# The bias of 128 exponentials on ScalarE: a constant in the instruction instead of a one-column tile

## The chip, the cores and the metric

The kernel runs on one core of a Trainium2 chip. A core has five engines that run side by side and meet only through semaphores: TensorE (matrix products, PE in the profile; its weight loads are PEld), VectorE (DVE), ScalarE (ACT), GpSimd (POOL) and SyncE (SP), which here only issues transfers. Data lie in SBUF (128 partitions) and in PSUM, the banks that TensorE writes. The metric is the device time of one execution in microseconds, as the median of several runs; the profile is of one execution, and its span is a little shorter than the timed run.

## The reference

`x` is 4096 x 64, `adj` is 4096 x 4096 with zeros and ones, and there are a 64 x 64 weight and a bias.

```python
h = jnp.maximum(_layernorm(x, axis=-1), 0.0)
support = h @ weight
mask = (adj != 0).astype(support.dtype)
rank = jnp.cumsum(mask, axis=1)
deg = rank[:, -1:]
k = jnp.minimum(deg, 100.0)
pos = rank - (deg - k)
w = mask * jnp.where(pos > 0, 0.5 ** (k - pos), 0.0)
return x + w @ support + bias
```

So every row of `adj` weights its neighbours by powers of one half. The last neighbours of a row count most when it has over 100 of them, and the exponent of a neighbour is the number of neighbours that follow it in its row (less an excess over 100). The matrix, 64 MB, has to be read once.

## The kernel before

The columns of `adj` are handled in two halves, right one first, since the exponents are counts from the right. The 4096 rows are 32 row tiles of 128; four row tiles make a group (8 groups), and a group with one half of the columns is a *unit* (16 units, 0 to 15). A unit is loaded as four transfers of 1 MB (128 rows x 2048 columns), 64 in all, numbered 0 to 63, all issued from one queue (L120) into a ring of eight buffers.

What becomes of a tile and of a unit, with the names of the functions and the lines that the profile shows:

- *convert* (L341 on VectorE; for tiles 1, 7 and 15 L339 on ScalarE): the ones and zeros become bytes, four matrix columns to a 32-bit word.
- *transpose* (L352, TensorE) turns the words, *settle* (L363, VectorE; L361 for the three tiles above) copies them from PSUM to the tile `mt`.
- *totals* (L369, TensorE) counts neighbours in each run of columns. *split* (L379, ScalarE) and *divide* (L382, VectorE) take two bytes of the counts into one tile `sums`; divide waits for split. *carry* (L388, GpSimd) adds what the right half counted.
- *suffix* (L396, TensorE) sums the counts from the right, and *clamp* (L400, VectorE) limits them.
- *place* (u, a) (L407 and L412, TensorE) makes the exponents of four blocks k of unit u: four products of L407, then sixteen of L412 that finish the four PSUM tiles `v` together. `v` is a ring of five buffers, so the fourth tile of a place can only be begun when the third tile of the place before has been read.
- *weigh* (u, k) (L420, ScalarE) reads two bytes of each word of `v` and writes 2 to the power of minus (byte + 38), 128 x 1024 numbers, to `wk`. This is the exponential. In the last unit, blocks 5, 6 and 7 are weighed in two halves of 128 x 512 each. There are 122 full and 6 half exponentials.
- For three blocks near the end, (14, 4), (15, 0) and (15, 4), VectorE builds the powers instead: *encode* (L426) and *take* (L431); *lower* (L439, GpSimd) prepares the other factor, and their aggregate is called *gather*.
- *aggregate* (L453, TensorE) multiplies `wk` with the rows of `support` in two parts (`hr`) and adds to `acc`, one PSUM tile per group.
- *drain* (L469, ScalarE; L467 on VectorE for the last quarter), *turn_back* (L476, TensorE) and *finish* (L483 and L484, VectorE) bring the sums into rows and add `x`. Two large stores and two small ones write the result (L491, L486).

Ahead of this stands a set-up with the normalisation of `x`, the product with the weight and the small constants. One of them is the tile `floor`, 128 x 1, filled once by GpSimd with -38 ln 2 (L192 and L193).

The order of the work on each engine is written out ahead: a planner at the end of the kernel holds for every task a rank, an estimated duration and its needs, and sorts all tasks into one list. Each engine runs its part of the list in that order and waits by semaphores where an input is not there yet. The estimates (1000 ns for a full exponential, 570 for a half) are not changed by the edit, so the order isn't either.

The line in question is the last one of weigh:

Of the kernel before, what the change touches and what calls it, by code (L numbers as in the profile page):

```python
# [15 lines left out]
U8 = mybir.dt.uint8  # L16
AF = mybir.ActivationFunctionType
# [10 lines left out]
LN2 = 0.6931471805599453  # L28
# [3 lines left out]
def kernel(  # L32
# [34 lines left out]
    nc = tc.nc  # L67
# [124 lines left out]
    floor = const.tile([P, 1], F32, name="floor")  # L192
# [135 lines left out]
    low, codes, masks, words, wts, accs, tots, pts, sums8, behind, vs, signed = {}, {}, {}, {}, {}, {}, {}, {}, {}, {}, {}, (1, 7, 15)  # L328
# [86 lines left out]
    def weigh(u, k, part=None):  # L415
        r = slice(0, W) if part is None else slice(part * W // 2, (part + 1) * W // 2)
        if not part:
            wts[u, k] = wpool.tile([P, 2, W], F32R, name="wk")
        v = vs[u, k] if part == 0 else vs.pop((u, k))
        nc.scalar.activation(wts[u, k][:, :, r], v.bitcast(U8).rearrange("p (i f) -> p f i", f=4)[:, :2, r], AF.Exp, scale=-LN2, bias=floor)  # L420

    def encode(u, k):

# [150 lines left out]
    for u, (g, c0, cb) in enumerate(UNITS):  # L574
# [9 lines left out]
        for k in range(2 * cb):  # L584
            due = at + k
            if k % 4 == 0:
                task(place, (u, k // 4), PE, due, 800, 920, [("clamp", u), ("constants", 1)], ("v", *(("encode" if (u, k + j) in QUICK else "weigh", u, k + j, *((1,) if u == U - 1 and k + j in PARTED else ())) for j in range(4))))
            if u == U - 1 and k in PARTED:
                continue
            weighs = "weigh"  # L590
            piece_of = block(u, k) // (HB // 2)
            if (u, k) in QUICK:
                weighs = "take"
                task(encode, (u, k), DVE, due - 8, 1160, 1300, [("place", u, k // 4), ("convert", NT - 2)])
                task(take, (u, k), DVE, due - 8, 690, 820, [("encode", u, k)], ("w", ("gather", u, k)))
                task(lower, (u, k), POOL, due - 8, 1200, 1300, [("second", piece_of // 2, piece_of % 2), ("convert", NT - 3)])
            else:
                task(weigh, (u, k), ACT, due + 2.5, 1000, 1130, [("place", u, k // 4)], ("w", ("aggregate", u, k)))
            task(gather if (u, k) in QUICK else aggregate, (u, k), PE, due + 14, 480, 720, [(weighs, u, k), ("lower", u, k) if (u, k) in QUICK else None, ("second", piece_of // 2, piece_of % 2)] +
                 ([("drain", g - 1)] if g and head and k == 0 else []))  # L600
        for part in range(2 if u == U - 1 else 0):
            for k in PARTED:
                due = at + k + part
                task(weigh, (u, k, part), ACT, due + 2.5, 570, 700, [("place", u, k // 4)], None if part else ("w", ("aggregate", u, k, 1)))
                task(aggregate, (u, k, part), PE, due + 14, 260, 500, [("weigh", u, k, part)])
# [20 lines left out]
    while kinds:  # L626
        heads = []
        for kind, keys in kinds.items():
            f, args, engine, rank, hold, lag, needs, pool = tasks[keys[0]]
# [10 lines left out]
        f, args, _, _, hold, lag, _, pool = tasks[key]  # L640
# [54 lines left out]
```

## Time and profile before

| | before |
|---|---|
| time, median of 3 runs | 192.47 us (192.40 to 192.48) |
| span of the profiled execution | 190.5 us |
| TensorE busy | 170.0 us (89%) |
| VectorE busy | 161.6 us (85%) |
| ScalarE busy | 160.0 us (84%) |
| exponentials, L420 | 128, 130.5 us busy, 1106 ns mean |
| read from memory | 68.2 MB, 363 GB/s over the span |

Busy time on an engine is the sum of its reported durations; neighbours overlap a little on ScalarE and VectorE, so that a reported duration is longer than the time for which an instruction keeps the engine from the next one. Two instructions back to back tell the latter by the distance of their starts. Where lines of a timeline are shown, the columns are the start in us from the beginning of the span, the length in us of the (merged) piece, engine, line, operation, output and input, shapes and number of instructions; in square brackets stands the idle time just ahead and what ended it. In tables of stretches the columns are: the stretch in us, its length, the busy time of PE, PEld, DVE, ACT and POOL with their numbers of instructions, the granted TensorE clock, the busy share of the 16 DMA engines, and GB/s.

### The profile page before, as it was taken

The page shows a single profiled execution, that of the slowest core. Times are in us where ns is not written, and L with a number is a line of the kernel's source. Part 1 is how long each engine was busy: PE and PEld are TensorE (multiplying, and loading weights), DVE is VectorE, ACT ScalarE, POOL GpSimd, SP SyncE. Part 2 cuts the span into 40 slices and gives each one's busy share as a digit, 9 for nine tenths or more (in the row PEclk, how much of TensorE's full clock was granted, in tenths as well). Part 3 has the DMA queues.
Part 4 walks back from the last instruction along what each step waited for, and adds up shares of the span by engine and source line. Part 5 has one row for each costly group of instructions (what it writes and reads, how often), then busy time and mean ns, then how long its engine had stood idle before and what let it go on. Part 6 is the DMA issues. An engine that isn't in the chain of part 4 may idle for free.

```text
span 190.5 us, 3798 instructions
## 1 busy us (share of the span) xinstructions
PE 170.0 (89%) x1499; PEld 105.3 (55%) x1499; DVE 161.6 (85%) x221; ACT 160.0 (84%) x176; POOL 20.0 (10%) x60
## 2 busy tenths in 40 slices
PE   7779878899979999999899989998898989999980
PEld 5657646465636564556466545563554455655460
DVE  4834886999999999999998999989879879996633
ACT  2298248699999997999998989798977998999980
POOL 7000062300001000100100010000100029001000
PEclk9999999999999999999999999999999999999996
DMA  6999999999999999999999999999999999912000
GB/s 201 420 427 420 415 423 421 418 413 427 420 413 425 420 415 425 420 416 425 420 413 427 420 415 427 418 416 425 418 411 428 418 415 425 381 40 83 0 3 28
DMA packets 10338, 69.49 MB, mean 365 GB/s; under 512 B 1360, under 2 KB 1616, under 8 KB 2128
## 3 DMA queue, kind: packets, MB, share of 16 engines
q1 hardware_dynamic: 10016, 69.15, 87.9%
q8 instruction: 12, 0.20, 0.4%
q10 hardware_dynamic: 304, 0.10, 0.2%
q14 instruction: 6, 0.05, 0.1%
HBM read 68.19 MB, written 1.05 MB: 363 GB/s over the span
## 4 chain that ended last, share of the span: by engine, by line
PE 33%; DVE 33%; DMA 20%; ACT 6%; POOL 3%; issue 2%; POOLq 0%; ACTq 0%; DVEq 0%
DMA a_sb<-in_adj_dram 20%; DVE m L341 16%; PE acc L453 11%; PE pt L352 6%; DVE mt L363 6%; ACT wk L420 4%; PE v L407 3%; PE v L412 3%; PE tot L369 2%; DVE behind L400 2%; DVE sums L382 2%; PE pc L265 1%; PE ps L396 1%; ACT mt L260 1%; DVE xs L307 1%
## 5 line engine op out<-in xcount | busy, mean ns | idle before, releaser
L420 ACT ACTIVATE wk<-v,floor 128x1024 fp32r<-128x1024 uint8 (+1 forms) x128 | 130.5, 1106 | 8.6 <-PE v L412 8.6
L341 DVE TENSOR_SCALAR m<-a_sb 128x2048 uint8<-128x2048 f32 x61 | 84.6, 1391 | 7.1 <-DMA a_sb<-in_adj_dram 7.1
L453 PE MATMUL acc<-wk,hr 128*128 128x512 f32 (+1 forms) x256 | 79.1, 424 | 1.7 <-ACT wk L420 1.1
L453 PEld LDWEIGHTS acc<-wk,hr 128*128 128x128 f32 x256 | 43.1, 188 | 21.0 <-ACT wk L420 6.7
L352 PE MATMUL pt<-ident,m 128*128 128x128 f32 x256 | 39.8, 279 | 7.6 <-DVE m L341 6.3
L363 DVE COPY mt<-pt 128x512 uint32<-128x512 uint32 x61 | 41.3, 680 | 3.8 <-PE pt L352 3.7
L352 PEld LDWEIGHTS pt<-ident,m 128*128 128x128 f32 x256 | 28.9, 141 | 21.8 <-PE acc L453 4.7
L388 POOL COPY sums<-behind 1x512 f16<-1x512 f16 x8 | 6.4, 798 | 132.8 <-ACT sums L379 132.8
L407 PE MATMUL v<-behind,where 32*128 32x512 f16 x128 | 14.8, 383 | 1.8 <-ACT wk L420 0.9
L412 PE MATMUL v<-mt,tri 32*32 32x512 f16 x512 | 14.3, 395 | 0.0
L379 ACT ACTIVATE sums<-tot 128x512 f16<-128x512 uint8 x16 | 9.6, 602 | 2.9 <-PE tot L369 2.8
L382 DVE CAST sums<-tot 128x512 f16<-128x512 uint8 x16 | 10.9, 680 | 1.3 <-ACT sums L379 1.3
L400 DVE TENSOR_SCALAR behind<-ps,excess 128x512 f16<-128x512 f32 x16 | 11.8, 738 | 0.1
L369 PE MATMUL tot<-mt,band 128*32 128x512 f16 x128 | 10.2, 393 | 0.3 <-DVE mt L363 0.3
L412 PEld LDWEIGHTS <-tri 32*32 32x32 f16 x512 | 4.4, 88 | 10.4 <-issue 10.4
L396 PE MATMUL ps<-sums,later 128*128 128x512 f16 x32 | 9.6, 381 | 0.5 <-DVE sums L382 0.5
L407 PEld LDWEIGHTS <-where 32*128 32x128 f16 x128 | 3.7, 91 | 10.0 <-issue 9.3
L339 ACT ACTIVATE m<-a_sb 128x2048 int8<-128x2048 f32 x3 | 7.7, 2560 | 1.2 <-DMA a_sb<-in_adj_dram 1.1
L248 PE MATMUL none<-junk 128*128 128x256 bf16 x44 | 7.6, 351 | 1.1 <-DVE junk L133 1.1
L260 ACT ACTIVATE mt<-px 64x512 f32<-64x512 f32 x8 | 4.2, 586 | 4.8 <-PE px L256 4.8
L248 PEld LDWEIGHTS <-junk 128*128 128x128 bf16 x44 | 5.5, 126 | 3.3 <-DVE junk L133 1.1
L469 ACT ACTIVATE acc_sb<-acc,bias_sb 128x512 f32<-128x512 f32 (+1 forms) x8 | 5.3, 665 | 0.8 <-PE acc L453 0.8
(87 smaller groups left out, 94.1 us busy)
## 6 DMA issues: line engine op xcount, KB each, us to landing
a_sb<-in_adj_dram SPq DMA_DIRECT2D x64, 1024.0 KB, 17.6
xr<-in_x_dram SPq DMA_DIRECT2D x2, 512.0 KB, 6.4
out_dram<-xr SPq DMA_DIRECT2D x1, 512.0 KB, 17.8
out_dram<-xr SPq DMA_DIRECT2D x1, 384.0 KB, 2.3
out_dram<-xr ACTq DMA_DIRECT2D x1, 64.0 KB, 1.6
out_dram<-xr SPq DMA_DIRECT2D x1, 64.0 KB, 1.6
w<-in_L_gnn_weight_dram ACTq DMA_DIRECT2D x2, 16.0 KB, 6.1
bias_sb<-in_L_gnn_bias_dram SPq DMA_DIRECT2D x1, 0.2 KB, 15.9
```

The costliest lines, as they stand in the source:

```text
L248: nc.tensor.matmul(none[:, :2 * P], junk[:, :P], junk, start=True, stop=True)
L341: nc.vector.tensor_scalar(m_v, a_v, 0.0, 64.0, op0=ALU.not_equal, op1=ALU.add)
L352: nc.tensor.transpose(pts[n][:, c, :], m32[:, c * P:(c + 1) * P], ident)
L363: nc.vector.tensor_copy(mw, pt)
L369: nc.tensor.matmul(tot[SUB * c:SUB * (c + 1), :], band[:, SUB - 12 - 4 * a:2 * SUB - 12 - 4 * a], masks[u][:, c, :, a], start=(a == 0), st ...
L382: nc.vector.tensor_copy(*bytes_of(u, 1))
L396: nc.tensor.matmul(px, later[cb][:r, f, :], sums[:r, f, :], start=(f == 0), stop=(f == 1))
L400: nc.vector.tensor_scalar(behind[u], pts.pop((u, "s")), excess[UNITS[u][2]], float(MAX_NEIGH), op0=ALU.subtract, op1=ALU.min)
L407: nc.tensor.matmul(v, where[q, a, :], behind[u][q, :], start=True, stop=False, skip_group_check=True)
L412: nc.tensor.matmul(vs[u, 4 * a + j][SUB * c:SUB * (c + 1), :], tri[q, q], m, start=False, stop=True, skip_group_check=True)
L420: nc.scalar.activation(wts[u, k][:, :, r], v.bitcast(U8).rearrange("p (i f) -> p f i", f=4)[:, :2, r], AF.Exp, scale=-LN2, bias=floor)
L453: nc.tensor.matmul(accs[g][:, r], parts.rearrange("p s d -> p (s d)"), wk[:, s, r], start=(k == s == 0 and c0 + cb * E * P == N), stop=(c0 ...
```

## The change

The activation instruction computes func(scale x input + bias). Its bias can be a column of SBUF with one number for each partition, or a number in the instruction itself. Before, the exponential had the tile `floor`, whose 128 numbers are all -38 ln 2. After, the same number is written into the instruction. The purpose is that ScalarE has one operand less to fetch in each of 128 instructions.

```diff
-        nc.scalar.activation(wts[u, k][:, :, r], v.bitcast(U8).rearrange("p (i f) -> p f i", f=4)[:, :2, r], AF.Exp, scale=-LN2, bias=floor)
+        nc.scalar.activation(wts[u, k][:, :, r], v.bitcast(U8).rearrange("p (i f) -> p f i", f=4)[:, :2, r], AF.Exp, scale=-LN2, bias=-38.0 * LN2)
```

The tile `floor` and its filling stay in the program, unread. Nothing else is edited.

## The prediction

> **What bounds the kernel now.** I read the page's first two parts, then busy time by stretches around the end of the loads, then ScalarE's groups, then the timelines of VectorE and ScalarE from 144 us on, and last the chain of waits in the same stretch.
>
> ```profile
> PE 170.0 (89%) x1499; PEld 105.3 (55%) x1499; DVE 161.6 (85%) x221; ACT 160.0 (84%) x176; POOL 20.0 (10%) x60
> ...
> DMA  6999999999999999999999999999999999912000
> ...
> 160.00:165.00 5.00, 4.78 (x57) 2.85 (x56) 5.00 (x6) 4.37 (x5) 1.85 (x2) 1.00 1.02 424
> 165.00:167.00 2.00, 2.00 (x29) 1.21 (x26) 2.00 (x4) 1.80 (x3) 0.00 (x0) 1.00 0.74 303
> 167.00:168.00 1.00, 1.00 (x5) 0.64 (x4) 1.00 (x2) 1.00 (x2) 0.00 (x0) 1.00 0.19 78
> ```
>
> The first line tempts: ScalarE is 84% busy and the change makes most of its instructions shorter. The second decides: the 16 DMA engines are full from the first slices to about 165 us (share 1.02 at 424 GB/s just before). 64 loads of 1 MB arrive, one each 2.48 us by the landing events of the trace, the last at 167.96 us. No faster engine moves that. So the kernel is a load stream of 168 us and a tail of 22.5 us; only what shortens the tail counts. Three engines are nearly full beside the stream, so one must also ask which of them is late when it ends.
>
> ```profile
> 155.91 0.69 DVE L382 CAST sums<-tot 128x512 f16<-128x512 uint8 x1 [0.86 <-ACT sums L379]
> ...
> 163.87 1.39 DVE L341 TENSOR_SCALAR m<-a_sb 128x2048 uint8<-128x2048 f32 x1
> ...
> 166.34 1.38 DVE L341 TENSOR_SCALAR m<-a_sb 128x2048 uint8<-128x2048 f32 x1
> ...
> 168.87 1.39 DVE L341 TENSOR_SCALAR m<-a_sb 128x2048 uint8<-128x2048 f32 x1
> ```
>
> This is VectorE's timeline. L341 converts a landed tile. The last three convert at 163.87, 166.34 and 168.87 us what landed at 163.00, 165.48 and 167.96: VectorE is 0.9 us behind the stream, and after 155.91 it has no idle time until the last conversion. That idle time of 0.86 us at 155.91 is a wait for ScalarE: divide (L382) may not start before split (L379) of the same unit has ended.
>
> ```profile
> 146.61 6.19 ACT L420 ACTIVATE wk<-v,floor 128x1024 fp32r<-128x1024 uint8 x6 [1.26 <-PE v L412]
> 152.69 0.69 ACT L469 ACTIVATE acc_sb<-acc,bias_sb 128x512 f32<-128x512 f32 x1
> 153.26 2.13 ACT L420 ACTIVATE wk<-v,floor 128x1024 fp32r<-128x1024 uint8 x2
> 155.25 0.62 ACT L379 ACTIVATE sums<-tot 128x512 f16<-128x512 uint8 x1
> ...
> 165.56 6.19 ACT L420 ACTIVATE wk<-v,floor 128x1024 fp32r<-128x1024 uint8 x6 [0.20 <-PE v L412]
> 171.64 0.69 ACT L469 ACTIVATE acc_sb<-acc,bias_sb 128x512 f32<-128x512 f32 x1
> 172.21 1.12 ACT L420 ACTIVATE wk<-v,floor 128x1024 fp32r<-128x1024 uint8 x1
> 173.21 0.61 ACT L379 ACTIVATE sums<-tot 128x512 f16<-128x512 uint8 x1
> 173.68 10.80 ACT L420 ACTIVATE wk<-v,floor 128x1024 fp32r<-128x1024 uint8 x13
> 184.50 0.47 ACT L469 ACTIVATE acc_sb<-acc,bias_sb 128x256 f32<-128x256 f32 x1
> ```
>
> ScalarE's timeline: eight exponentials (L420) in the queue ahead of that late split, and from 165.56 us to the drain (L469) at 184.50 us no idle time at all: 20 exponentials, two other instructions. So ScalarE bounds at two places that count: ahead of 155.25, and in the tail. The chain of waits puts 33% on TensorE, 33% on VectorE and 20% on the loads, and only 6% on ScalarE, since it names whoever came last at each step; near the end it has these lines, with the last five half exponentials on the path:
>
> ```profile
> 181.04 0.46 issue
> 181.49 2.99 ACT wk L420 x5
> 184.48 0.02 issue
> 184.50 0.48 ACT acc_sb L469
> ```
>
> **What the Trainium skill says.** "ScalarE: Activation LUTs", section "What ACT_TABLE_LOAD costs": an activation with constant scale and bias takes 186 ns + 0.833 ns per element, each one-column operand adds about 93 ns, and neighbours overlap by about 93 ns. The trace agrees with the form: 128x1024 with the tile has a median of 1118 ns (280 + 853 = 1133 by the page). "ScalarE activation tables: per-element evaluation and per-set limits", section "What a function is on this engine", says that with the same operands an instruction costs the same whatever the function. The trace agrees: half exponentials and drains, both 512 wide with a bias tile, start 570 and 569 ns ahead of their successor. No page says whether the 93 ns are seen by the next instruction or vanish in the overlap. "Perfetto Trace Analysis", section "Per-instruction lifecycle", says that the reported window runs from the start in the ALUs to the acknowledged write, so the distance of starts is the better measure of what an instruction occupies. I use that.
>
> **The change part by part.** *The operand.* Distances from one start to the next, back to back, in the trace before: exponential of 1024 with the tile 998 ns (median of 90); of 512 with the tile 570; drain of 512 with a bias tile 569; split of 512 (Copy, no tile) 475; turned and relu of 512 (no tile) 477. So at equal width the tile occupies 94 ns, as the page's 93. I take 94 ns: a full exponential goes from 998 to 904 ns, a half from 570 to 476, and the mean reported time of the 128 from 1106 to about 1012 ns. Over 128 that is 12.0 us of ScalarE. Most of it lies beside the full load stream and turns into waits of L420 for L412.
>
> *The tile itself.* The memset of floor stays and is unread (109 ns on GpSimd at 5 us, far ahead of use). The first exponential loses its wait on GpSimd, met 25 us earlier. The order on each engine is otherwise the same; a wait of TensorE on ScalarE stands one instruction group earlier in the set-up (L304 instead of the next L407), on work long done. All of it: 0.
>
> *Ahead of the tail.* Split at 155.25 has eight exponentials before it since ScalarE last waited: 8 x 0.094 = 0.75 us, and 0.07 us more of a small wait on v inside the six: 0.8 us earlier. Its counts (L369) have their last start at 153.21, so they don't hold it. Divide's wait of 0.86 us shrinks by as much, and everything on VectorE after it moves 0.8 us earlier, as does TensorE, whose L407 at 154.44 waits for the exponential of 153.26. The limit is the stream: conversions can move up 0.87 us before they meet their landing. So 0.8 us fits, just.
>
> *In the tail, all 0.8 us earlier to begin with:* exponentials of unit 13 from 164.77. Four at 0.904 end their turn at 168.39; the next needs v of place (14,0), at 169.64 - 0.8 = 168.83. One more to 169.74, one to 170.64: drain. 0.57 later exp (14,2) at 171.21; split of unit 15 at 172.11 (was 173.21; its counts are there at 171.65). Exp (14,3) at 172.59, then three more until 176.2. TensorE: turn_back needs totals and drain: 171.57, then an aggregate; L407 of place (14,1) at 172.5 (was 173.44, -0.94). The order on TensorE (L412, two aggregates, suffix) carries -0.94 to suffix, clamp and place (15,0): L407 at 175.72, v ready at 176.73. Exp (15,1) thus starts at 176.75 instead of 177.81 (-1.06), after half a microsecond of a new wait. The fourth L407 of place (15,1) waits for the end of exp (15,2), the v ring having five buffers: -1.06 - 0.09 - 0.09, so -1.25 at 178.73; v follows 0.93 later, and the half exponentials begin at 179.66 instead of 180.91. Six at 0.476 need 2.86 us where they took 3.59. But VectorE's encode and take of block (15,4) start at the same v and need 2.02 us, to 181.59; gather and two pairs of half aggregates follow on TensorE (1.35 us before, 0.1 of it a wait for ScalarE). Drain at 181.59 + 1.25 + 0.03 = 182.87 instead of 184.50: -1.63. From drain to the end (5.97 us) nothing changes.
>
> Sum: 0.8 (VectorE's late start made good) + 0.8 (tail). 192.47 - 1.6 = 190.9 us.
>
> **The rivals.** (a) *VectorE's lead is lost again.* Another wait between 145 and 160 us, for instance VectorE on transposes (0.57 us at 148.99), takes the place of the one for split. Then the tail starts where it did: place (15,0) gains 0.1 to 0.2, two exponentials 0.19, the end 0.1, together about 0.45 us: 192.0. For it: three engines are nearly full here. Against: in that stretch TensorE's own waits are for L420 and for VectorE. (b) *Only the reported duration shrinks*, the distance of starts stays at 998 ns, the operand read being hidden in the overlap: 192.47, no change. Against it stand 475 and 569 ns for equal widths. (c) *ScalarE bounds throughout* and 12 us come off: 180.5. Against: the last load lands at 167.96 and 64 MB at the measured rate can't come sooner. Its reasonable remnant is a tail bound by ScalarE alone: 20 x 0.094 = 1.9 plus the 0.87 that the stream allows: 189.7. (d) *Slower:* earlier exponentials shift waits and thereby the store of 512 KB that shares the queue with the last loads, or TensorE's reads collide with VectorE's; the conversions already vary from 1.28 to 1.60 us. Six late conversions at 0.1 more would cost 0.6 us without the gain: 193.1. Against: the order on every engine is kept, and an instruction that gets shorter in a fixed order makes none start later by its waits.
>
> **How the numbers follow.** My forecast (a gain of 1.1 to 2.1) has 0.70; (a), gains of 0.4 to 1.1, 0.14; more than 2.1 (towards 189.7) 0.08; (b) 0.04; (d) 0.04. The likeliest gives 190.9. The range takes in the greater part of (a) and half of the greater gains: 190.1 to 192.0. Faster by over 0.2% (0.38 us): 0.70 + 0.14 + 0.08 = 0.92; same 0.04; slower 0.04.
>
> **What would show it.** Right: L420's mean near 1012 ns and back-to-back starts 904 ns apart; ScalarE's busy time near 148 us, with L420's wait for L412 growing from 8.6 us to some 18; the last load landing at 168 as before; the wait of divide for split at 156 all but gone and the last conversion near 168.1; suffix of unit 15 near 174.3; drain near 182.9. Wrong: starts still 998 apart (rival b); the last conversion still at 168.9 (rival a); another wait before place (15,0).

## The result, and the profile after

| | before | after | forecast |
|---|---|---|---|
| median time | 192.44 us (4 runs) | 190.76 us (190.50 to 191.04, 4 runs) | 190.9 us |
| ratio, 95% interval | | 0.992 (0.989 to 0.995) | 0.992 |
| L420: mean; start to start, full / half | 1106; 998 / 570 ns | 1015; 906 / 479 ns | 1012; 904 / 476 ns |
| L420 waiting for L412 | 8.6 us | 14.9 us | some 18 us |
| last load landed | 167.96 us | 167.85 us | 168 us |
| last conversion begins | 168.87 us | 167.94 us | 168.1 us |
| drain of the last group begins | 184.50 us | 182.81 us | 182.9 us |

The kernel is 1.7 us faster. The distances of starts and the landings are read from the trace's single instructions and landing events, the other places from the views below. In two of the experiments below one execution of six fell in a slower state of the chip, with a lower granted clock, and is left out of the medians. The group of the exponentials, from the page of the kernel after:

```profile
L420 ACT ACTIVATE wk<-v 128x1024 fp32r<-128x1024 uint8 (+1 forms) x128 | 120.0, 1015 | 15.3 <-PE v L412 14.9
```

`floor` is gone from the inputs. (The 120.0 us count the time in which two neighbours overlap once; the sum of the durations, which busy time was called above, would be 128 x 1015 ns, 129.9 us.) Busy time fell by 10.5 us (130.5 before) and the wait for `v` grew by 6.3: most of what ScalarE saved, it waits. What reached the end is seen in VectorE's timeline of the kernel after:

```profile
154.76 0.69 DVE L382 CAST sums<-tot 128x512 f16<-128x512 uint8 x1 [0.18 <-ACT sums L379]
...
162.91 1.40 DVE L341 TENSOR_SCALAR m<-a_sb 128x2048 uint8<-128x2048 f32 x1
...
165.40 1.40 DVE L341 TENSOR_SCALAR m<-a_sb 128x2048 uint8<-128x2048 f32 x1
...
167.94 1.39 DVE L341 TENSOR_SCALAR m<-a_sb 128x2048 uint8<-128x2048 f32 x1
```

Divide's wait for split is 0.18 us (0.86 before), and the last three conversions follow their landings (162.89, 165.37, 167.85 us) by 0.02 to 0.09 us, where they followed by 0.9. VectorE has caught up with the load stream. And ScalarE's timeline of the kernel after:

```profile
168.40 1.94 ACT L420 ACTIVATE wk<-v 128x1024 fp32r<-128x1024 uint8 x2 [0.21 <-PE v L412]
170.60 0.69 ACT L469 ACTIVATE acc_sb<-acc,bias_sb 128x512 f32<-128x512 f32 x1 [0.26 <-PE acc L453]
171.19 1.02 ACT L420 ACTIVATE wk<-v 128x1024 fp32r<-128x1024 uint8 x1
172.09 0.60 ACT L379 ACTIVATE sums<-tot 128x512 f16<-128x512 uint8 x1
172.57 3.78 ACT L420 ACTIVATE wk<-v 128x1024 fp32r<-128x1024 uint8 x4
176.67 5.97 ACT L420 ACTIVATE wk<-v 128x1024 fp32r<-128x1024 uint8 x9 [0.32 <-PE v L412]
182.81 0.47 ACT L469 ACTIVATE acc_sb<-acc,bias_sb 128x256 f32<-128x256 f32 x1 [0.17 <-PE acc L453]
```

The tail that ran without a gap before now has four waits for TensorE, up to 0.32 us each. The chain of waits of the kernel after says the same from the other side:

```profile
143.64 19.25 DMA a_sb<-in_adj_dram
162.89 0.02 issue
162.91 1.40 DVE m L341
...
179.41 3.37 PE acc L453 x18
182.78 0.02 issue
182.81 0.48 ACT acc_sb L469
```

From 143.64 to 162.89 us the loads are on it, and just ahead of the drain stand 3.37 us of aggregates, where the kernel before had five half exponentials. From the loads to the drain no exponential is left on the chain. In the kernel before, the queue ahead of divide of unit 13 was on it as well:

```profile
153.38 2.01 ACT wk L420 x2
155.39 0.49 ACT sums L379
155.88 0.02 issue
155.91 0.69 DVE sums L382
```

The two profiles differ in one more thing, the granted TensorE clock. The page of the kernel after has, in 40 slices of 4.7 us:

```profile
PEclk9999687999999999999999999999999999999998
```

The clock record gives half the clock from 20.47 to 23.88 us and from 27.29 to 30.71, while the kernel before had none until its last 4 us. The last load lands at nearly the same time in both, and the kernel with 28 constants (below) reaches the end of its loads and its tail at the same distances without such a stretch (0.07 and 14.88 us, where this one has 0.09 and 14.87). So this early difference is not where the gain comes from.

### The profile page after: what moved, and what is told of

It is laid out like the page before. It is cut to its first block, busy times and chain, and to the rows that moved or that the text cites. A ratio compares the mean times of both kernels' runs of the same rounds, so it can differ in the third digit from the quotient of the medians.

```text
span 188.8 us, 3797 instructions
## 1 busy us (share of the span) xinstructions
PE 171.8 (91%) x1499; PEld 107.7 (57%) x1499; DVE 161.7 (86%) x221; ACT 149.5 (79%) x176; POOL 20.4 (11%) x60
## 4 chain that ended last, share of the span: by engine, by line
PE 49%; DVE 29%; DMA 10%; ACT 5%; POOL 3%; issue 2%; POOLq 0%; ACTq 0%; DVEq 0%
PE acc L453 18%; DVE m L341 13%; DMA a_sb<-in_adj_dram 10%; PE pt L352 10%; DVE mt L363 6%; PE v L412 4%; PE v L407 4%; ACT wk L420 3%; PE pc L265 2%; PE tot L369 2%; PE pd L281 2%; PE ps L396 2%; DVE behind L400 2%; PE po L476 2%; ACT mt L260 1%
## 5 line engine op out<-in xcount | busy, mean ns | idle before, releaser
L420 ACT ACTIVATE wk<-v 128x1024 fp32r<-128x1024 uint8 (+1 forms) x128 | 120.0, 1015 | 15.3 <-PE v L412 14.9
L453 PE MATMUL acc<-wk,hr 128*128 128x512 f32 (+1 forms) x256 | 77.7, 421 | 1.1 <-ACT acc_sb L469 0.6
L352 PE MATMUL pt<-ident,m 128*128 128x128 f32 x256 | 41.2, 286 | 6.0 <-DVE m L341 5.4
L352 PEld LDWEIGHTS pt<-ident,m 128*128 128x128 f32 x256 | 29.7, 145 | 20.6 <-PE acc L453 4.8
L407 PE MATMUL v<-behind,where 32*128 32x512 f16 x128 | 13.7, 383 | 1.5 <-DVE behind L400 1.1
L412 PE MATMUL v<-mt,tri 32*32 32x512 f16 x512 | 14.2, 394 | 0.0
L369 PE MATMUL tot<-mt,band 128*32 128x512 f16 x128 | 10.2, 393 | 0.3 <-DVE mt L363 0.3
L407 PEld LDWEIGHTS <-where 32*128 32x128 f16 x128 | 3.7, 90 | 10.3 <-issue 9.8
L412 PEld LDWEIGHTS <-tri 32*32 32x32 f16 x512 | 4.4, 88 | 8.7 <-issue 8.7
L272 ACT ACTIVATE xs<-pc 128x512 f32<-128x512 f32 x4 | 2.3, 610 | 6.0 <-PE pc L265 6.0
```

The costliest lines, as they stand in the source:

```text
L352: nc.tensor.transpose(pts[n][:, c, :], m32[:, c * P:(c + 1) * P], ident)
L369: nc.tensor.matmul(tot[SUB * c:SUB * (c + 1), :], band[:, SUB - 12 - 4 * a:2 * SUB - 12 - 4 * a], masks[u][:, c, :, a], start=(a == 0), st ...
L407: nc.tensor.matmul(v, where[q, a, :], behind[u][q, :], start=True, stop=False, skip_group_check=True)
L412: nc.tensor.matmul(vs[u, 4 * a + j][SUB * c:SUB * (c + 1), :], tri[q, q], m, start=False, stop=True, skip_group_check=True)
L453: nc.tensor.matmul(accs[g][:, r], parts.rearrange("p s d -> p (s d)"), wk[:, s, r], start=(k == s == 0 and c0 + cb * E * P == N), stop=(c0 ...
```

## The experiments

The theory: the 94 ns count at two places only, in the eight exponentials queued ahead of split of unit 13 (they bring VectorE to the end of the stream in time) and in the 20 of the tail. Rivals: all of it is the shorter tail (T), or the gain goes with ScalarE's total work (W). Times are medians of each kernel, with the kernel before on the same chip beside it; a bracket after a ratio is its 95% interval. The ratio is estimated from all runs and can differ a little from the quotient of the medians. For each profile I give three places: landing of the last load, start of the last conversion, start of the last group's drain by ScalarE.

### The gain by place: four subsets of the 128

The edit is the condition under which the constant stands in place of the tile, over (unit, block):

```diff
-AF.Exp, scale=-LN2, bias=floor)
+AF.Exp, scale=-LN2, bias=-38.0 * LN2 if (u, k) >= (13, 4) else floor)                      # tail, 20
+AF.Exp, scale=-LN2, bias=-38.0 * LN2 if (11, 4) <= (u, k) < (12, 4) else floor)            # lead, 8
+... if (11, 4) <= (u, k) < (12, 4) or (u, k) >= (13, 4) else floor)                        # both, 28
+... if (u, k) < (11, 4) or (12, 4) <= (u, k) < (13, 4) else floor)                         # the other 100
```

> Constant bias only in the last 20 exponentials, from (13, 4) on; the other 108 keep the tile. My theory (half of the gain is VectorE's late start made good ahead of the tail, half is the tail itself): divide of unit 13 still waits some 0.9 us for split near 155.9, the last conversion stays at 168.9, and the tail gives only about 0.45 us, because the counts of unit 15 come no earlier: about 192.0. Rival T (all the gain is the shorter tail, 20 times 94 ns less a little): about 190.8, the same as with all 128.

> Constant bias only in the eight exponentials (11, 4) to (12, 3), those in ScalarE's queue ahead of split of unit 13. My theory: split starts about 0.8 us earlier, divide's wait of 0.86 us goes, every later conversion moves up by 0.8 to 0.9 us until it meets its landing, and the whole tail follows with its old length: about 191.6. Rival T: the tail is untouched, so 192.4. Rival W (the gain belongs to ScalarE's total work): 8 of 128, so 192.3.

> The two sets together, 28 of 128. My theory: the whole gain, 190.8. Rival T: also 190.8, but then e1 alone gives it. Rival W: 28 of 128 of 1.7 us, so 192.1.

> The complement: constant bias in the other 100, the tile in those 28. My theory: 9.4 us of ScalarE's work saved beside a full load stream, all of it turned into waits for v; time as before, 192.4, within 0.2. Rival W: 100 of 128 of 1.7 us, so 191.1.

| constant in | time | before | ratio | landing | last conversion | drain | behind the landing | conversion to drain |
|---|---|---|---|---|---|---|---|---|
| none (before) | 192.44 | | 1 | 167.96 | 168.87 | 184.50 | 0.91 | 15.63 |
| tail, 20 | 191.53 | 192.29 | 0.9957 (0.9937 to 0.9977) | 167.88 | 168.53 | 183.38 | 0.65 | 14.85 |
| lead, 8 | 191.67 | 192.29 | 0.9962 (0.9949 to 0.9975) | 167.67 | 167.74 | 183.29 | 0.07 | 15.55 |
| both, 28 | 190.93 | 192.29 | 0.9928 (0.9903 to 0.9954) | 168.26 | 168.33 | 183.21 | 0.07 | 14.88 |
| other 100 | 192.12 | 192.29 | 0.9993 (0.9981 to 1.0006) | 167.83 | 168.29 | 183.93 | 0.46 | 15.64 |
| all 128 (after) | 190.76 | 192.44 | 0.992 (0.989 to 0.995) | 167.85 | 167.94 | 182.81 | 0.09 | 14.87 |

The medians give -0.76 us for the tail's 20, -0.62 for the lead's 8, -1.36 for both (the sum is -1.38) and -0.17 for the other 100, which their interval (0.37 us faster to 0.12 slower) can't tell from nothing. 28 exponentials carry the gain; over three quarters of the instructions made shorter, 100 times 92 ns or 9.2 us of ScalarE's work, bring 0.17 us or nothing. That refutes W, and T as well: the tail alone gives about half. The last two columns show the two parts separately. Conversion to drain takes 15.6 us with the tile in the tail and 14.9 with the constant, whatever stands in the lead. The distance behind the landing is 0.07 to 0.09 us with the constant in the lead and 0.46 to 0.91 without. This second part varies from one execution to the next: in the kernel of the next section that moves the column to the scale, whose exponentials are as long as those before, the last conversion stands 1.55 us behind its landing (167.90), while conversion to drain takes 15.66.

```profile
169.45 1.38 DVE L341 TENSOR_SCALAR m<-a_sb 128x2048 uint8<-128x2048 f32 x1
```

So one trace shows that VectorE has caught up, but not what this is worth; that is in the medians.

VectorE in the kernel with the constant in the eight of the lead alone:

```profile
154.38 0.68 DVE L382 CAST sums<-tot 128x512 f16<-128x512 uint8 x1
...
162.74 1.37 DVE L341 TENSOR_SCALAR m<-a_sb 128x2048 uint8<-128x2048 f32 x1 [0.48 <-DMA a_sb<-in_adj_dram]
...
167.74 1.40 DVE L341 TENSOR_SCALAR m<-a_sb 128x2048 uint8<-128x2048 f32 x1
```

Divide has no wait left (no bracket), and at 162.74 us VectorE waits for the load itself, 0.48 us. That is where the gain of the lead ends: the stream allows no more. Not all of the earlier start is due to the eight exponentials, though. In this execution they also began earlier, at 145.52 us where the kernel before had 146.61, with the tile in every exponential ahead of them in both:

```profile
145.52 5.75 ACT L420 ACTIVATE wk<-v 128x1024 fp32r<-128x1024 uint8 x6 [0.24 <-PE v L412]
```

With the constant in the tail's 20 alone the same line of VectorE still has its wait:

```profile
155.56 0.69 DVE L382 CAST sums<-tot 128x512 f16<-128x512 uint8 x1 [0.88 <-ACT sums L379]
```

My figure for the tail alone, 0.45 us, was too small; it measured 0.76. And I had the last conversion at 168.9; it stands at 168.53, 0.65 us behind its landing, within the variation just named.

### The price of a column operand: moved, and doubled

```diff
-    nc.gpsimd.memset(floor, -38.0 * LN2)
+    nc.gpsimd.memset(floor, -38.0 * LN2); slope = const.tile([P, 1], F32, name="slope"); nc.gpsimd.memset(slope, -LN2)
...
-AF.Exp, scale=-LN2, bias=floor)
+AF.Exp, scale=slope, bias=-38.0 * LN2)      # moved
+AF.Exp, scale=slope, bias=floor)            # both
```

> The one-column operand is moved, not removed: the bias is the constant, and the scale is read from a 128 x 1 tile filled with -ln 2. If a column operand costs its 94 ns whichever it is: starts 998 ns apart and the time of the kernel before, 192.3. If the cost belongs to the bias alone: 904 ns and 190.8.

> Scale and bias both from tiles. If the operands add: starts 1092 ns apart. Then split of unit 13 comes another 0.75 us later and VectorE with it (last conversion near 169.6), and the 20 exponentials of the tail, which ScalarE already ran without a gap, take 1.9 us more: about 194.9. If two operands are fetched side by side: 998 ns and 192.3.

| column operands | full, start to start | half | time | before | ratio |
|---|---|---|---|---|---|
| none (after) | 906 ns | 479 ns | 190.76 | 192.44 | 0.992 |
| bias (before) | 998 ns | 570 ns | 192.44 | | 1 |
| scale | 1001 ns | 570 ns | 192.40 | 192.45 | 1.000 (0.999 to 1.001) |
| bias and scale | 1093 ns | 665 ns | 196.75 | 192.45 | 1.026 (1.022 to 1.029) |

A column costs 91 to 95 ns, the same for scale as for bias and the same for 512 as for 1024 elements, and two add. The time does not go along: the first column cost 1.7 us, the second 4.3 by the medians (196.47 to 198.69 in five runs; 4.2 to 5.7 by the interval), where I expected 2.65, 0.75 ahead of the tail and 1.9 in it. The kernel with both shows where, in VectorE's timeline:

```profile
158.64 0.69 DVE L382 CAST sums<-tot 128x512 f16<-128x512 uint8 x1 [1.50 <-ACT sums L379]
...
171.58 1.36 DVE L341 TENSOR_SCALAR m<-a_sb 128x2048 uint8<-128x2048 f32 x1
```

Its page counts 1.9 us of waiting for `v` in the whole run, where the kernel before had 8.6. So ScalarE has little slack left in which it could catch up: the eight exponentials ahead of split of unit 13 begin at 148.64 us, where the kernels with one column in all exponentials up to there have 145.5 to 147.2, and split follows 9.3 us behind instead of 8.6. Divide of unit 13 waits 1.50 us. The last conversion stands 3.37 us behind its landing (171.58 after 168.21), 2.5 more than in the trace before; I had allowed 0.75. The tail takes 17.2 us (188.79 - 171.58), 1.6 more; I had 1.9. The two make 4.1 us, as much as this execution (196.47 us) took longer than the profiled one of the kernel before (192.40). That the backlog comes from the lost slack is read from this one trace; no run takes it apart.

### Only the wait of divide: split of unit 13 ahead of two exponentials

The kernel before, with the written order changed at one place on ScalarE:

```diff
-    for at, _, f, args in sorted(order, key=lambda o: o[:2]):
+    order.sort(key=lambda o: o[:2]); ahead = [o for o in order if o[2:] in ((totals, (13,)), (split, (13,)))]; late = [o for o in order if o[2:] in ((weigh, (12, 2)), (weigh, (12, 3)))]; at13 = order.index(ahead[0]); order = [o for o in order[:at13] if o not in late] + ahead + [o for o in late if o in order[:at13]] + [o for o in order[at13:] if o not in ahead]
+    for at, _, f, args in order:
```

> The kernel before (tile as bias), but ScalarE runs split of unit 13 ahead of exponentials (12, 2) and (12, 3) instead of after them; nothing else changes its order. Divide then need not wait: its idle time of 0.86 us near 155.9 goes. If that wait alone held VectorE back: last conversion near 168.0 and 191.6. My theory says that TensorE waits for exponential (12, 2) too (the fourth L407 of place (12, 1)), and now 0.48 us longer, so that turn_back and with it finish on VectorE come 0.4 us later: last conversion near 169.3, about 192.7.

It took 194.32 us against 192.45 (ratio 1.009, 1.006 to 1.011): slower, and by more than I said (192.7). VectorE, in this kernel:

```profile
154.95 0.70 DVE L382 CAST sums<-tot 128x512 f16<-128x512 uint8 x1
158.44 0.43 DVE L483 TENSOR_TENSOR xr<-po,xr 128x256 f32<-128x256 f32 x1 [2.79 <-PE po L476]
...
170.71 1.39 DVE L341 TENSOR_SCALAR m<-a_sb 128x2048 uint8<-128x2048 f32 x1
```

Divide starts without waiting, 0.96 us earlier than before. Finish behind it then waits 2.79 us for turn_back. The chain of waits of this kernel names the way there:

```profile
153.42 0.31 issue
153.73 0.60 ACT sums L379
154.33 1.02 ACT wk L420
155.35 0.04 issue
155.39 0.42 PE v L407
155.81 0.58 PE v L412 x16
156.40 1.15 PE acc L453 x2
157.55 0.85 PE po L476 x4
```

Split has to wait 0.31 us, which the view calls issue; the last product of its counts (L369) ends 0.09 us ahead of its start. Exponential (12, 2) starts at 154.23 instead of 153.26, and the fourth L407 at 155.39 instead of 154.44. That much is the step as I had it, 0.95 us in place of 0.48. Then TensorE itself takes longer: two aggregates 1.15 us, 0.47 elsewhere, and turn_back 0.85 where the kernel before had 0.60. The stretches of this kernel show the reason in the column after POOL's, the granted clock:

```profile
154.00:155.40 1.40, 0.01 (x1) 0.00 (x0) 1.40 (x2) 1.40 (x3) 1.01 (x1) 1.00 1.00 415
155.40:156.40 1.00, 1.00 (x18) 0.22 (x17) 0.25 (x1) 0.94 (x1) 1.00 (x3) 0.59 1.04 434
156.40:157.50 1.10, 1.10 (x3) 0.80 (x4) 0.00 (x0) 0.96 (x1) 1.10 (x3) 0.50 0.96 387
```

TensorE had nothing to do for 1.4 us, and soon after it ran at half its clock, for 3.4 us by the trace's clock record (155.59 to 159.00); in the kernel before the clock is 1.00 throughout this stretch. So the later finish has two parts, the late exponential and a slow TensorE. An estimate tells them apart: in the kernel before, turn_back ended 1.85 us after the fourth L407 had begun (156.28 after 154.43). With the same 1.85 us, finish could have begun at about 157.3 instead of 156.51, so 0.8 us of its delay belong to the exponential and 1.2 to the clock. Four of the five runs took 194.28 to 194.36 us and one 192.94, near the 192.7 that I had without the clock; there is no trace of that one.

It is tempting to say that the pause brought the clock down. The runs don't show it. Half clock for 3.41 or 10.24 us is on record between 20 and 32 us in seven of the ten profiles, and in five of these (the kernel after is one) TensorE was busy throughout the 3.4 us just ahead. And a pause of 1.26 us at 180.71 us in the kernel of the next part, or one of 2.08 us at 5.60 in the kernel with the constant in the tail, was followed by the full clock. The cause stays open.

What the run does settle: removing the wait that stood in the view is not what helped, since by the estimate finish would have come later at full clock too. Near 155.9 us VectorE is held by two results of one queue, split and the exponential that frees `v`. The second is seen on TensorE in the kernel before:

```profile
154.43 0.37 PE L407 MATMUL v<-behind,where 32*128 32x512 f16 x1 [0.52 <-ACT wk L420]
```

Shorter exponentials bring both.

### The planner told of the shorter exponential

```diff
-task(weigh, (u, k), ACT, due + 2.5, 1000, 1130, ...)
+task(weigh, (u, k), ACT, due + 2.5, 906, 1040, ...)
-task(weigh, (u, k, part), ACT, due + 2.5, 570, 700, ...)
+task(weigh, (u, k, part), ACT, due + 2.5, 476, 610, ...)
```

> The kernel after, with the planner told of it: the estimate of an exponential is 906 ns instead of 1000, of a half 476 instead of 570. The planner then writes another order on all engines, and the ranks were fitted to the old one. If the order before was held back by the old estimates: faster than 190.8. If the fit of the ranks is worth more than right estimates: between 191 and 193. I expect the second.

194.21 us against 192.45 of the kernel before on that chip (ratio 1.010, 1.007 to 1.012), so slower than the 191 to 193 that I had given, and some 3.4 us slower than the same exponentials in the old order. VectorE's line of divide has a wait of 1.42 us for split at 155.50 us, and the last conversion is at 171.81 us, 3.75 behind its landing. The order comes out otherwise on TensorE, VectorE and ScalarE; which of its changes costs most wasn't tried.

No run was faster than the kernel after; 28 constants measured 190.93 us, the same within what the runs can tell.

## Why the prediction was right, point by point

- *What bounds.* The load stream ends at 167.85 us after, 167.96 before; in all profiles of subsets between 167.67 and 168.26. It gave the frame, and 100 of 128 shorter exponentials beside it brought nothing that could be measured.
- *The operand.* 94 ns by comparison of equal widths in the trace before; 92 (full) and 91 (half) measured. The price of about 93 ns that the Trainium skill gives ("ScalarE: Activation LUTs", section "What ACT_TABLE_LOAD costs") would have left open whether it shows in the distance of starts. In this trace it does, with 92 and 91 ns. The reported duration fell by the same amount (1106 to 1015 ns).
- *Ahead of the tail.* I had split, and VectorE with it, 0.8 us earlier, all of it from the eight exponentials. In the trace divide moved by 1.15 us (155.91 to 154.76). The eight gave 0.64 of it, since split came 8.00 us after their start and not 8.64. They also began 0.52 us earlier (146.09 instead of 146.61), which my sum had not, and by which executions of equal instructions differ too. The last conversion moved by 0.93, of which 0.11 is the landing itself: the stream allowed no more. The mechanism was right and so was its limit. That my 0.8 came so near to 0.93 is due to the limit, since the parts were off: 0.64 for the 0.8, and 0.52 that I had left out. In so far it was luck. With the lead alone the time fell by 0.62 us.
- *In the tail.* 0.8 us forecast; conversion to drain shrank by 0.76 (15.63 to 14.87). The way there was as traced: exponential (15, 1) started at 176.67 (forecast 176.75) after a new wait of 0.32 us, the half exponentials at 179.6 (179.66), the drain at 182.81 (182.87), held at the end by TensorE and not by ScalarE.
- *Rivals.* (a), VectorE's lead lost again, did not come; its size was wrong too (0.45 against 0.76 measured for the tail alone). The trace with the constant in the tail shows the term: from its last conversion, exponential (15, 1) started 0.22 us earlier than before and the half exponentials 0.40, as I had them (0.1 to 0.2, and 0.19 for two exponentials), but the drain 0.78. The end, for which I carried 0.1 here, gave 0.38, as much as in my forecast for the whole change. (b) fell with 906 ns, (c) with the other 100. (d), slower by collisions, did not show: conversions took 1.38 to 1.61 us in the end of the run, as before.
- *A size that was off.* ScalarE's wait for `v` grew by 6.3 us, not by 9. Another 1.7 of the 10.5 us of busy time saved are no longer in the span. The rest stands against other waits of ScalarE, and 1.7 us of these have nothing to do with the change: L272 in the set-up waited 6.0 us instead of 4.3, ahead of the first exponential, because the two products of L265 took 1.83 us at half clock and not 1.02.

## What to carry to other kernels

When a stream of loads fills the run, an instruction made shorter pays only in the queue ahead of something that is late when the stream ends, and in the tail; find those two stretches and count the instructions there, not the total. A wait in the view shows one of the results that a late queue delays: before one reorders to remove it, look for the others from the same queue. And a queue that is nearly full is not linear: 92 ns taken from each exponential gained 1.7 us, 95 ns added cost 4.3 or more.

## What the runs showed of the hardware

A one-column operand of an activation costs its 91 to 95 ns also when it is the scale, and two columns cost twice that (998, 1001 and 1093 ns from start to start at 128 x 1024). In the ten profiles TensorE was granted half its clock for stretches of 3.41 or 10.24 us: between 20 and 32 us in seven of them, and in mid-run only once, at 155.59 us in the kernel with split moved ahead, 0.2 us after it had resumed from a pause of 1.44 us (all ten also end at half clock). Two aggregates then took 1.15 us and not 0.47. The early stretches reached neither the last landing (167.67 to 168.26 us in the profiles of the subsets) nor the length of the tail; the late one made finish some 1.2 us later, by the estimate above. What starts such a stretch is not shown.
